# Spare buffers in an edge sort and the pace of an interleaved attention, in a graph-transformer layer

## The chip, the cores and the metric

The kernel runs on one core of one Trainium2 chip. The metric is the device time of one execution in microseconds; the figure given for a kernel is the median of its runs. The core has a tensor engine (TensorE, PE; its weight loads are listed as PEld), a vector engine (VectorE, DVE), a scalar engine (ScalarE, ACT), GpSimd (POOL) and a sync engine (SP) that here only issues transfers.

## The reference

A layer of a graph transformer over 6250 nodes of 256 features and 206,250 directed edges (100,000 drawn, both ways round, and a loop at every node). Cut to what matters:

```python
xn = layernorm(x)
# graph attention, 4 heads of 64
h  = xn @ W;  el = h @ Wl.T;  er = h @ Wr.T
e  = exp(leaky_relu(el[src] + er[dst], 0.2))
w  = e / segment_sum(e, src)[src]
g  = elu(stack_h(segment_sum(w[:, h] * h[dst], src)) + b)
# linear attention, 4 heads of 32, with 4 memory keys and values
q, k, v = split(rmsnorm(xn) @ w_qkv)
m  = rmsnorm((softmax(q) * scale) @ (softmax_n([mem_k, k]).T @ [mem_v, v]) @ w_out + b_out) + xn
x  = x + g + m
# mixture of 8 experts, the best 2 of each token
t  = layernorm(x)
x  = x + t + sum_e(combine[:, e] * (gelu(t @ w1[e] + b1[e]) @ w2[e] + b2[e]))
```

## The kernel before

The nodes are 49 tiles of 128 (NT); the edges lie as 1612 columns of 128 (EC). The work falls into two stages.

**Sort and projections.** The edges have to be brought into the order of their source nodes. `sort_batch` (L364) takes 32 columns at a time, 51 batches in all. Each batch goes through a chain over three engines:

- DVE writes the one-hot `ob` of each edge's pair of node tiles (L381); 32 small matmuls count them into the PSUM tile `n_ps` (L389); a scan on DVE makes running counts `inc` (L393), and a product spreads them into `ahead` (L406).
- Four matmuls give every edge its rank, into `r_ps` (L413, L414), a tile of two PSUM banks. DVE takes the maximum over it into `rank` (L421), and ACT rounds it into `rank2` (L433).
- DVE writes the edges' values times the one-hots into `rv` (two instructions at L438) and the one-hot of the rank, `ohp` (L442), 4096 elements to a partition, the longest instruction of a batch. 32 matmuls over `ohp` and `rv` pack the batch into `g_ps` (L448), and ACT copies it into `grid` (L453).

The SBUF tiles of a batch come from the pool `sortw`, which holds two of each name (`ahead` one); the PSUM tiles of the sort, `n_ps`, `r_ps` and `g_ps`, come from a pool that holds one of each. The projections (`project`, L297) of 13 groups of up to four node tiles run among the first 39 batches: layer norm on ACT and DVE, transposes and matmuls on PE into the PSUM tiles `tp` and `pr` (L337, L342). They write the `table` in HBM that the edges will be gathered from. The last twelve batches run beside `context` (L461), the softmax over all keys and its product with the values. The PSUM pools of this stage are closed at L554 to L556, and the next stage opens its own: among them a one-bank tile `bank` (L840), into which two constants are copied (L850, L851).

**Edges, attention and experts.** For every pair of node tiles, `pack` (L860) brings the edges of the pair into slots, 35 columns to a node tile, and makes the rows `dst_x` to be gathered. `gather` (L949) then issues 35 indirect transfers on POOL into a tile `xe`, of which there are three. When a tile's rows have landed, `weights` (L996) makes the edges' weights, and `sums` (L1009), in four parts, adds the weighted rows into `a_ps` on PE; `look` (L960) prepares the one-hots of the next tile.

The loop of this stage (L1051 to L1076) goes over the node tiles in blocks: nine of four tiles, then smaller ones of 3, 2, 2, 2, 1, 1, 1 and 1. After each of a tile's four parts it calls `some_more` (L1031), which takes one turn (or, in the smaller blocks, as many as it takes to be through at the end of the block) from a list `todo`. First in that list is the `attention` (L568): three turns for each of 13 groups, 39 in all. When the attention has ended, `open_experts` (L624) loads the experts' weights and opens the pool `W["fw"]`; from then on the list holds the `finish_steps` (L654) of the blocks that are through with their sums, each of 11 turns: `front`, `route` and nine turns of expert matmuls (L764, L780). The order of the instructions on each engine is fixed when the program is built.

Of the kernel before, what the change touches and what calls it, by code (L numbers as in the profile page):

```python
# [8 lines left out]
F32 = mybir.dt.float32  # L9
F16 = mybir.dt.float16  # L10
# [7 lines left out]
P = 128  # L18
# [3 lines left out]
BW = 2 * CB  # L22
# [13 lines left out]
def tile_gps_layer(  # L36
# [43 lines left out]
    NB = NQ + NQ % 2  # L80
    BB = min(CB, 512 // NB)
# [116 lines left out]
    def pairs(ap):  # L198

        names = "abcd"[:len(ap.shape) - 2]  # L200
        spaced = " ".join(names)
        return ap.rearrange(f"p {spaced} (n two) -> p {spaced} n two", two=2)
# [11 lines left out]
    sps = sx.enter_context(tc.tile_pool(name="sortp", bufs=1, space=PSUM))  # L214
# [143 lines left out]
    sw = sw_ctx.enter_context(tc.tile_pool(name="sortw", bufs=2))  # L358

    def flat(t):  # L360
        return t.rearrange("p a b -> p (a b)")


    def sort_batch(t):  # L364
        c0 = t * BW
        w = min(BW, EC - c0)
        cs = slice(c0, c0 + w)
        ends = [min(w, a + CB) for a in range(0, w, CB)]
        nb = len(ends)
        bs = slice(t * (BW // CB), t * (BW // CB) + nb)  # L370

        def two(a, n):

            return a[:, :, None, :].to_broadcast([a.shape[0], w, n, 2])

        def row(a, n):

            return pairs(a)[:, None].to_broadcast([a.shape[0], w, n, 2])

        ob = sw.tile([P, BW, NB], F16, name="ob")  # L380
        nc.vector.tensor_tensor(  # L381
            pairs(ob[:, :w]), two(bid[:, cs], NB // 2), row(iota_h[:, :NB], NB // 2),
            op=OP.is_equal,
        )


        n_ps = sps.tile([NB, BW, 2], F32, name="n_ps")
        for c in range(w):
            nc.tensor.matmul(  # L389
                n_ps[:, c, :], lhsT=ob[:, c, :], rhs=one_none, start=True, stop=True  # L390
            )
        inc = sw.tile([NB, BW, 2], F16, name="inc")
        nc.vector.tensor_tensor_scan(  # L393
            flat(inc[:, :w]), starts.rearrange("q b c two -> q (b c two)")[:, :2 * w],
            flat(n_ps[:, :w]), 0.0, op0=OP.mult, op1=OP.add,
        )
        if w == BW:
            nc.scalar.copy(
                ntot[:, bs],
                inc[:NQ].rearrange("q (b c) two -> q b c two", c=CB)[:, :, CB - 1, 0],  # L400
            )
        else:
            for b, e in enumerate(ends):
                nc.scalar.copy(ntot[:, bs][:, b:b + 1], inc[:NQ, e - 1, 0:1])
        ahead = sw.tile([NB, BW, NB], F16, name="ahead", bufs=1)
        nc.vector.tensor_tensor(  # L406
            pairs(ahead[:, :w]), two(inc[:, :w], NB // 2), row(delta, NB // 2), op=OP.mult
        )
        r_ps = sps.tile([P, BW // BB, 512], F32, name="r_ps")
        for i, a in enumerate(range(0, w, BB)):  # L410
            z = min(w, a + BB)
            part = r_ps[:, i, :(z - a) * NB]
            nc.tensor.matmul(part, lhsT=upto_own, rhs=flat(ob[:, a:z]), start=True, stop=False)  # L413
            nc.tensor.matmul(  # L414
                part, lhsT=ones16[:NB, :], rhs=flat(ahead[:, a:z]), start=False, stop=True
            )

        rank = sw.tile([P, BW], F32, name="rank")
        nf = w // BB
        if nf:  # L420
            nc.vector.tensor_reduce(  # L421
                rank[:, :nf * BB].rearrange("p (i c) -> p i c", c=BB),
                r_ps[:, :nf, :BB * NB].rearrange("p i (c b) -> p i c b", b=NB),
                axis=AX.X, op=OP.max,
            )
        if w > nf * BB:
            nc.vector.tensor_reduce(
                rank[:, nf * BB:w],
                r_ps[:, nf, :(w - nf * BB) * NB].rearrange("p (c b) -> p c b", b=NB),
                axis=AX.X, op=OP.max,  # L430
            )
        rank2 = sw.tile([P, BW, 2], F16, name="rank2")
        nc.scalar.activation(  # L433
            rank2[:, :w], rank[:, :w, None].to_broadcast([P, w, 2]), AF.Identity, bias=less_own
        )
        rv = sw.tile([P, BW, 2, NB], F16, name="rv")
        for i, v in enumerate((va, vb)):
            nc.vector.tensor_tensor(  # L438
                pairs(rv[:, :w, i, :]), pairs(ob[:, :w]), two(v[:, cs], NB // 2), op=OP.mult
            )  # L440
        ohp = sw.tile([P, BW, P], F16, name="ohp")
        nc.vector.tensor_tensor(  # L442
            pairs(ohp[:, :w]), two(rank2[:, :w], P // 2), row(iota_h, P // 2), op=OP.is_equal
        )
        g_ps = sps.tile([P, BW // CB, 2, NB], F32, name="g_ps")
        for b, e in enumerate(ends):
            for c in range(b * CB, e):
                nc.tensor.matmul(  # L448
                    flat(g_ps[:, b]), lhsT=ohp[:, c, :], rhs=flat(rv[:, c]),
                    start=(c == b * CB), stop=(c == e - 1),  # L450
                )
        for i in range(2):
            nc.scalar.copy(  # L453
                grid[:, :, bs, i, :],
                g_ps[:, :nb, i, :NQ, None].to_broadcast([P, nb, NQ, 2]).rearrange(
                    "p b q two -> p q b two"
                ),
            )
# [61 lines left out]
    for t0, n in groups:  # L520
        project(t0, n)
        for _ in range(3):
            sort_batch(batches.pop(0))
# [15 lines left out]
    while batches:  # L539
        sort_batch(batches.pop(0))  # L540
        next(steps, None)
# [80 lines left out]
    W = {}  # L622
# [191 lines left out]
    def heads(x2_j, sums, weights):  # L814

        ri = held_pool[0].tile([P, H], F32, name="ri")
        nc.vector.tensor_scalar_max(ri, weights, 1e-12)
        nc.vector.reciprocal(ri, ri)
        nc.vector.tensor_tensor(
            x2_j.rearrange("p (h f) -> p h f", h=H), sums,  # L820
            ri[:, :, None].to_broadcast([P, H, FO]), op=OP.mult,
        )
# [173 lines left out]
    def weights(xe, e_ps):  # L996
        z = gw.tile([P, CPT, H], F32, name="z")
        nc.vector.tensor_reduce(
            z, e_ps[:, 1:].rearrange("p c i h -> p c h i"), axis=AX.X, op=OP.add
        )  # L1000

        tc.keep_in_program_order(nc.vector.tensor_add(z, z, xe[:, :, :H]))  # L1002
        nc.vector.scalar_tensor_tensor(z, z, 0.2, z, op0=OP.mult, op1=OP.max)
        ew = gw.tile([P, CPT, H], F32, name="ew")
        nc.scalar.activation(ew, z, AF.Exp)
        nc.vector.tensor_copy(ew_s, ew)
# [24 lines left out]
    def some_more(calls=None):  # L1031

        steps = 1 if calls is None else -(-sum(max(1, n) for _, n in todo) // calls)
        while todo and steps:
            try:
                next(todo[0][0])
                todo[0][1] -= 1
                steps -= 1
            except StopIteration:
                todo.pop(0)  # L1040
                if "fw" not in W:
                    qx.close()
                    open_experts()
# [7 lines left out]
    for t0, n in blocks:  # L1051
        x2 = gw.tile([P, GT, D], F32, name="x2", bufs=3)
        for j in range(n):
            b = t0 + j
            xe, _ = ready.pop(b)
            oh, e_ps = seen.pop(b)
            weights(xe, e_ps)
            a_ps = pa.tile([FO + 1, S, H, SN], F32, name="a_ps")
            for k in range(S):
                sums(k, oh, xe, a_ps)  # L1060
                if b + 1 < NT:
                    look(b + 1, k)
                if k == 1 and b % U == U - 1 and b + U + 1 < NT:
                    pack(b // U + 2)
                some_more(None if n == GT else (n - j) * S - k)
            a_s = gw.tile([FO + 1, H, S, SN], F32, name="a_s")
            nc.scalar.copy(a_s.rearrange("f h s n -> f s h n"), a_ps)  # L1067
            hd_ps = yps.tile([P, H, FO + 1], F32, name="y_ps")
            for h in range(H):
                nc.tensor.transpose(  # L1070
                    hd_ps[:, h, :], a_s[:, h].rearrange("f s n -> f (s n)"),
                    ident[:FO + 1, :FO + 1],
                )
            heads(x2[:, j, :], hd_ps[:, :, :FO], hd_ps[:, :, FO])
        rows_left = None if (t0 + n) * P <= N else last
        todo.append([finish_steps(hps, yps, x2, t0, n, rows_left, gb_s), NX + 3])  # L1076
# [28 lines left out]
    with tc.If(over_n > 0):  # L1105
        with ExitStack() as gx:
# [45 lines left out]
            with tc.tile_pool(name="allf", bufs=2) as fw, tc.tile_pool(  # L1152
                name="hp2", bufs=2, space=PSUM
# [63 lines left out]
```

## Time and profile before

| what | us |
|---|---|
| runs: median (lowest to highest) | 2762.55 (2759.88 to 2763.56), 3 runs |
| the profiled execution | 2760.09 |
| its span | 2758.0 |
| granted TensorE clock, mean | 0.82 |
| first gather (L952) starts | 443.9 |
| last gather ends | 2635.4 |
| busy: PE, DVE, POOL, ACT | 2108.4, 1939.9, 1688.5, 753.6 |

The profile shows one execution. Busy time of an engine is the time in which one of its instructions ran; a busy PE is not PE at its peak. A group line gives line, engine, operation, tiles written and read, count, then busy time and mean duration in ns, then the engine's idle time just before these instructions and what ended most of it ("<-"). "issue" is time in which the engine waited for nothing that the profile shows. In a list of waits, each line is: who waited, for whom, microseconds in total, how often, and the longest. This is the page's view of the span in 40 equal slices, each digit the busy share in tenths, and PEclk the clock granted to TensorE in tenths:

```profile
PE   6888664556465498969899889596895988887987
DVE  6877977668487668775879568765776676876742
POOL 1000204777777777777677777777777777777610
PEclk9878665666677599979999889698796999888887
```

A slice is 69 us. The first six or seven slices are the sort, the rest is the loop over the node tiles.

### The profile page before, as it was taken

To read this page: it belongs to the slowest core of one execution; us is meant where nothing else is said; L and a number is where in the kernel's file an instruction comes from. 1 tells how busy PE (TensorE), PEld (TensorE's weight loads), DVE (VectorE), ACT (ScalarE), POOL (GpSimd) and SP (SyncE) were. 2 spreads that over 40 slices of the span, in tenths; PEclk is the share of its full clock that TensorE was granted. 3 is DMA by queue.
4 is the path that set the end of the run, shared out by engine and by line. 5 is a ranking of instruction groups with operands and counts; after the bars stand their busy time and mean duration, and the time that the engine had idled before them with its cause. 6 is when DMAs were issued, how large, how long until landed. Compare 5 with 4: busy or idle time off the path is not lost.

```text
span 2758.0 us, 39898 instructions
## 1 busy us (share of the span) xinstructions
PE 2108.4 (76%) x15539; PEld 1584.8 (57%) x15539; DVE 1939.9 (70%) x3992; ACT 753.6 (27%) x1691; POOL 1688.5 (61%) x1779
## 2 busy tenths in 40 slices
PE   6888664556465498969899889596895988887987
PEld 3555442445354367656667667465675666666774
DVE  6877977668487668775879568765776676876742
ACT  4655311112231132213223222021221322232333
POOL 1000204777777777777677777777777777777610
PEclk9878665666677599979999889698796999888887
DMA  2110200222222422121212212212122221221110
GB/s 70 33 30 25 20 1 15 44 59 58 58 59 52 109 36 44 29 44 29 41 29 44 37 36 37 36 29 36 36 29 36 34 40 29 38 37 34 33 15 5
DMA packets 106775, 103.96 MB, mean 38 GB/s; under 512 B 42822, under 2 KB 78884, under 8 KB 106580
## 3 DMA queue, kind: packets, MB, share of 16 engines
q0 software_dynamic: 54880, 60.70, 14.6%
q1 hardware_dynamic: 50004, 39.75, 5.1%
q8 instruction: 124, 2.03, 0.3%
q10 hardware_dynamic: 1696, 0.89, 0.1%
q14 instruction: 71, 0.58, 0.1%
HBM read 86.57 MB, written 14.65 MB: 37 GB/s over the span
## 4 chain that ended last, share of the span: by engine, by line
POOL 29%; PE 26%; DVE 15%; issue 14%; ACT 2%; DMA 2%; DVEq 0%; ACTq 0%; POOLq 0%
POOL xe L952 28%; PE a_ps L1021 8%; PE h_ps L764 7%; PE y_ps L780 6%; DVE rc L914 4%; DVE ohp L919 3%; DVE ohc L907 2%; DMA xe<-table,dst_x 2%; PE y_ps L704 1%; DVE ohw L1014 1%; PE y_ps L755 1%; PE s_ps L924 1%; DVE x L784 1%; POOL kv L492 1%; PE y_ps L699 1%
## 5 line engine op out<-in xcount | busy, mean ns | idle before, releaser
L952 POOL DMA_INDIRECT xe<-table,dst_x x1715 | 1654.5, 965 | 632.7 <-issue 604.4
L1021 PE MATMUL a_ps<-ohw,xe 128*65 128x128 f32 x4410 | 552.1, 283 | 16.3 <-DVE ohw L1014 12.7
L1021 PEld LDWEIGHTS a_ps<-ohw,xe 128*65 128x65 f32 x4410 | 518.2, 144 | 50.9 <-DVE ohw L1014 19.2
L924 PE MATMUL s_ps<-rc,ohp 128*128 128x144 f16 x2525 | 257.4, 275 | 279.7 <-DVE ohp L919 279.6
L764 PE MATMUL h_ps<-tokT,w1s 128*128 128x512 f32 (+3 forms) x1088 | 431.3, 515 | 47.5 <-ACT hT L772 45.4
L924 PEld LDWEIGHTS <-ohp 128*128 128x128 f16 x2525 | 224.7, 121 | 342.9 <-DVE ohp L919 321.5
L780 PE MATMUL y_ps<-w2s,hT 128*128 128x256 f32 x1568 | 405.6, 390 | 0.0
L784 DVE SCALAR_TENSOR_TENSOR x<-y_ps,comb,x 128x256 f32<-128x256 f32 x392 | 189.0, 484 | 230.3 <-PE y_ps L780 230.0
L1014 DVE TENSOR_TENSOR ohw<-oh,bank 128x1280 f32<-128x1280 bf16 x196 | 323.4, 1650 | 32.3 <-PE a_ps L1021 30.8
L780 PEld LDWEIGHTS y_ps<-w2s,hT 128*128 128x128 f32 x1568 | 285.0, 193 | 66.3 <-issue 28.7
L772 ACT ACTIVATE hT<-h_ps,b1s 128x512 f32<-128x512 f32 (+3 forms) x272 | 154.4, 568 | 555.4 <-PE h_ps L764 412.1
L764 PEld LDWEIGHTS h_ps<-tokT,w1s 128*128 128x128 f32 x1088 | 193.6, 205 | 151.3 <-ACT hT L772 79.5
L914 DVE TENSOR_TENSOR rc<-ohc,bank 128x1152 f16<-128x1152 f16 (+1 forms) x350 | 228.0, 693 | 4.5 <-PE s_ps L924 0.7
L919 DVE TENSOR_TENSOR ohp<-to,bank 128x2048 f16<-128x2048 f16 (+1 forms) x175 | 195.1, 1115 | 0.0
L981 ACT COPY ohT<-t_ps 128x768 bf16<-128x768 bf16 x98 | 78.2, 798 | 319.0 <-PE t_ps L977 318.9
L1002 DVE TENSOR_TENSOR z<-z,xe 128x140 f32<-128x140 f32 x49 | 15.0, 307 | 210.6 <-DMA xe<-table,dst_x 202.5
L350 POOL COPY el<-tab 128x16 f32<-128x16 f32 (+1 forms) x13 | 3.5, 267 | 260.7 <-ACT tab L349 260.7
L907 DVE TENSOR_TENSOR ohc<-to,bank 128x1152 f16<-128x1152 f16 (+1 forms) x175 | 121.2, 692 | 0.4 <-ACT to L896 0.4
L442 DVE TENSOR_TENSOR ohp<-rank,iota_h 128x4096 f16<-128x4096 f16 (+1 forms) x51 | 116.1, 2277 | 6.3 <-ACT rank L433 6.0
L342 PE MATMUL pr<-wcat,xT 128*128 128x456 f32 x196 | 109.9, 691 | 5.9 <-ACT xT L339 5.9
L1067 ACT COPY a_s<-a_ps 65x512 f32<-65x512 f32 x49 | 28.4, 580 | 280.6 <-PE a_ps L1021 280.4
L448 PEld LDWEIGHTS <-ohp 128*128 128x128 f16 x1612 | 62.3, 109 | 56.4 <-DVE ohp L442 45.6
(269 smaller groups left out, 2483.9 us busy)
## 6 DMA issues: line engine op xcount, KB each, us to landing
xe<-table,dst_x POOLq DMA_INDIRECT x1715, 2.5
xt<-in_x_dram SPq DMA_DIRECT2D x24, 512.0 KB, 3.9
base_y<-xt SPq DMA_DIRECT2D x12, 512.0 KB
yt<-base_y SPq DMA_DIRECT2D x9, 512.0 KB, 4.4
out_dram<-x SPq DMA_DIRECT2D x9, 512.0 KB
w1s<-in_L_ffn_w_dram SPq DMA_DIRECT2D x8, 256.0 KB
w2s<-in_L_ffn_w_dram SPq DMA_DIRECT2D x8, 256.0 KB, 5.3
table<-tab SPq DMA_DIRECT2D x12, 138.0 KB
```

The source lines that it names most:

```text
L442: nc.vector.tensor_tensor(pairs(ohp[:, :w]), two(rank2[:, :w], P // 2), row(iota_h, P // 2), op=OP.is_equal)
L764: nc.tensor.matmul(h_ps[:, :w], lhsT=w1s[:, e, c, f * P:(f + 1) * P], rhs=held["tokT"][:, c, :w], start=(c == 0), stop=(c == DC - 1),)
L772: nc.scalar.activation(held[e][:, f, :w], h_ps[:, :w], AF.Gelu, bias=b1s[:, k:k + 1])
L780: nc.tensor.matmul(y_ps, lhsT=held[e][:, f, j * P:(j + 1) * P], rhs=w2s[:, e, f, :], start=(f == 0), stop=(f == FC - 1),)
L784: nc.vector.scalar_tensor_tensor(x2[:, j, :], y_ps, held["comb"][:, j, e:e + 1], x2[:, j, :], op0=OP.mult, op1=OP.add,)
L907: nc.vector.tensor_tensor(pairs(ohc[:, :m]), twos(to[:, 0, t0:t0 + m], U * CW // 2), iota_2[:, :, :U * CW // 2].to_broadcast([P, m, U * CW ...
L914: nc.vector.tensor_tensor(pairs(rc[:, :m, i, :]), pairs(ohc[:, :m]), twos(edges_q[:, t0:t0 + m, i, :], U * CW // 2), op=OP.mult,)
L919: nc.vector.tensor_tensor(pairs(ohp[:, :m]), twos(to[:, 1, t0:t0 + m], P // 2), iota_2.to_broadcast([P, m, P // 2, 2]), op=OP.is_equal,)
L924: nc.tensor.matmul(flat(s_ps), lhsT=ohp[:, t - t0, :], rhs=flat(rc[:, t - t0]), start=(t == 0), stop=(t == NBT - 1),)
L952: nc.gpsimd.indirect_dma_start(out=xe[:, c, :], out_offset=None, in_=table, in_offset=bass.IndirectOffsetOnAxis(ap=dst_x[:, c:c + 1], axis=0),
L1014: nc.vector.tensor_tensor(ohw[:, :n], oh[:, g0:g1, i, None, :].to_broadcast([P, n, H, SN]), ew_s[:, c0:c0 + n, :, None].to_broadcast([P, n ...
L1021: nc.tensor.matmul(a_ps[:, i].rearrange("f h n -> f (h n)"), lhsT=xe[:, c, H:], rhs=ohw[:, c - c0].rearrange("p h n -> p (h n)"), start=(c ...
```

## The change

Three tiles of the sort get one more buffer each: `r_ps` two instead of one, `rv` and `ohp` three instead of two. In the loop over the node tiles, `some_more` is called once more after the second and the fourth part of a tile for as long as the experts are not open, so that the attention takes three turns in every two calls instead of two. Nothing else is edited; no instruction is added or taken away.

```diff
-        r_ps = sps.tile([P, BW // BB, 512], F32, name="r_ps")
+        r_ps = sps.tile([P, BW // BB, 512], F32, name="r_ps", bufs=2)
...
-        rv = sw.tile([P, BW, 2, NB], F16, name="rv")
+        rv = sw.tile([P, BW, 2, NB], F16, name="rv", bufs=3)
...
-        ohp = sw.tile([P, BW, P], F16, name="ohp")
+        ohp = sw.tile([P, BW, P], F16, name="ohp", bufs=3)
...
                 some_more(None if n == GT else (n - j) * S - k)
+
+                if k % 2 and "fw" not in W:
+                    some_more()
```

## The prediction

> **What bounds the kernel now.** I read the page's busy shares and costliest groups first, then the timeline of GpSimd (POOL) alone, then the windows by stage, then the waits of the two parts of the sort, and last the timeline of all engines from tile to tile.
>
> ```profile
> PE 2108.4 (76%) x15539; PEld 1584.8 (57%) x15539; DVE 1939.9 (70%) x3992; ACT 753.6 (27%) x1691; POOL 1688.5 (61%) x1779
> L952 POOL DMA_INDIRECT xe<-table,dst_x x1715 | 1654.5, 965 | 632.7 <-issue 604.4
> ```
>
> By busy share TensorE leads. The second line says otherwise: 1715 gathers of 965 ns, and of POOL's 632.7 us of idle time before them 604.4 are "issue", that is, nothing the profile shows held them. The timeline of POOL tells what that issue is:
>
> ```profile
> 443.94 1.14 POOL L952 DMA_INDIRECT xe<-table,dst_x  x1 [95.74 <-issue]
> 448.15 0.94 POOL L952 DMA_INDIRECT xe<-table,dst_x  x1 [0.30 <-issue]
> ...
> 1344.57 0.94 POOL L952 DMA_INDIRECT xe<-table,dst_x  x1 [7.52 <-PE a_ps L1021]
> 2411.05 0.94 POOL L952 DMA_INDIRECT xe<-table,dst_x  x1 [2.60 <-PE a_ps L1021]
> 2592.04 0.94 POOL L952 DMA_INDIRECT xe<-table,dst_x  x1 [5.46 <-PE a_ps L1021]
> 2634.49 0.94 POOL L952 DMA_INDIRECT xe<-table,dst_x  x1 [0.30 <-issue]
> ```
>
> Each gather is followed by 0.30 us of its own issue, and in 2191 us (443.94 to 2635.4) the row is broken only three times, by 15.6 us in all, each time because a gather needed a buffer of xe whose tile was still in its sums (L1021). So the profiled execution of 2760.09 us is 443.9 us up to the first gather, 2191.5 us of gathers one behind the other, 122.6 us of rest after the last, and 2.1 us outside the span of 2758.0. It lies 2.5 us under the median of the runs (2762.55; 2759.88 to 2763.56). In the middle part only POOL's three waits can be won. What is taken from the first part moves the whole row of gathers, and with it the end, one for one.
>
> The first part is the sort (L364 to L458) to 409.7 us, when the last write of the grid starts, and then the first pack, 34 us of DVE work ahead of the first gather, which the change does not touch. How the sort runs:
>
> ```profile
> 100.00:200.00 100.00, 88.84 (x1091) 53.17 (x1090) 78.60 (x126) 61.23 (x241) 1.51 (x10) 0.83 0.12 35
> 200.00:300.00 100.00, 80.00 (x927) 47.07 (x925) 79.64 (x118) 51.87 (x200) 1.62 (x10) 0.81 0.25 30
> 300.00:400.00 100.00, 71.43 (x1021) 50.38 (x1020) 84.51 (x112) 23.21 (x72) 19.03 (x13) 0.62 0.01 2
> ```
>
> The columns are the window, its length, the busy time of PE, PEld, DVE, ACT and POOL, the granted clock, DMA share and GB/s. To 287 us, PE (with the projections of L342) and DVE are both near 80 to 89 with neither full; after it DVE leads. That is two engines that wait for each other in turn:
>
> ```profile
> DVE rv L438 <- PE g_ps L448: 39.7, 28, 4.6
> DVE ob L381 <- PE r_ps L413: 13.6, 10, 3.8
> PE g_ps L448 <- DVE ohp L442: 12.0, 12, 2.4
> PE tp L337 <- ACT xn L332: 5.6, 9, 0.6
> PE pr L342 <- ACT xT L339: 5.4, 12, 0.6
> PE r_ps L413 <- DVE rank L421: 4.1, 9, 0.5
> DVE rank L421 <- PE r_ps L414: 3.8, 6, 1.4
> ```
>
> These are the waits from 30 to 290 us (total, times, longest). The 39.7 us are rv's buffers: its third writer cannot start until the matmuls that read the first are done. From 290 to 410 us the same view has:
>
> ```profile
> PE g_ps L448 <- DVE ohp L442: 24.4, 13, 4.4
> PE r_ps L413 <- DVE rank L421: 13.2, 8, 10.8
> DVE ohp L442 <- ACT rank L433: 6.0, 2, 4.5
> DVE rank L421 <- PE r_ps L414: 5.5, 8, 0.9
> DVE rv L438 <- PE g_ps L448: 4.2, 4, 2.5
> ```
>
> **The change part by part.** No instruction is added or removed; three tags get one more buffer each, and turns of a list of work are taken earlier.
>
> Ranks' sums twice, and rv and ohp thrice, first stage (39 batches, 13 groups, some 21.2 us a group: one rv at 163.96, its like at 185.16). Inside a group PE runs without a gap for the first 11 us while DVE waits for it (2.15, 1.25 and 1.09 us); then DVE runs without a gap for 10 us while PE waits (0.46, 0.95 us, and 1.1 us for the projection's ACT). A third rv and ohp lets DVE go on for one batch's rv and ohp (0.59 + 0.58 + 2.29 = 3.5 us) during the first half, which is less work for it in the second, where PE stands. What goes is PE's waits for DVE: 12.0 + 4.1 = 16.1 us in the window. The 57 us that DVE waits (39.7 + 13.6 + 3.8) are not won, since PE, at 89 of 100, is next in line: late next is the projection's chain through ACT (5.6 + 5.4 us), which I leave in. Lower bound of the gain: nothing, if the engines' fixed order lets DVE only wait at the next instruction. Upper bound: PE also loses its half clock. In windows of 1 us the granted clock is 1.00 from 164 to 176 us and 0.50 from 177 to 183, and so on, group after group; the first projection of a group takes 3.0 us for four matmuls (at 181.28) where the next take 1.8; with g_ps at 1.57 instead of 1.00, r_ps at 0.52 instead of 0.34, and the transposes at 0.69 instead of 0.38, that is some 2.4 us a group, 29 us over 12 groups, so 45 us. DVE, busy 17.0 of 21.2 us, allows that (4.2 x 12 = 50). I take 16, the waits that are measured.
>
> Second part, twelve batches: DVE leads, so its own waits for the two buffers count: 5.5 + 4.2 = 9.7 us. The 6.0 us for ACT's rank stay (ACT was in the exponentials of L493), and so do the 11 us of the maximum at L462, which DVE does itself. Part of each wait only moves to the next one; between nothing and 9.7 I take 5.
>
> The sort's PSUM: tp, pr, n_ps, g_ps one bank each and r_ps two make six of eight; with r_ps twice all eight. The tile named bank is now filled from DVE at 18.60 and 18.85 us (0.22 and 0.18 us), in a bank that the sort does not use; after the change it must wait for one that the sort gives up, at its end on the path: +0.4 us. At best nothing.
>
> Three turns in every two calls, until the experts open. The attention's 39 turns take DVE 121 us, ACT 72 and PE 60 (sums of its groups), so 3.1, 1.9 and 1.5 us a turn; two more a tile are 6.2 us of DVE. What hides them: in tiles 0 to 6 DVE waits 22.2, 12.3, 11.2, 13.2, 0, 17.6 and 21.9 us for the gather (z at L1002), 14 us a tile. If that cover were gone they would make the sums later, but xe has three buffers: the sums of tile 5, the latest, end 7.9 us before the gather of tile 8 needs the buffer. Behind the extra turns stand the sums (k = 2 and the next tile's weights) on DVE and PE, and on SP the loads of xt and stores of base_y, the same in number. The 18 loads of the experts (152 GB/s from 940 to 968 us) come 13 calls, or 3.25 tiles of 44.7 us, earlier; POOL kept its pace under them (21.3 busy of 28 us, as everywhere).
>
> The experts' turns, 11 a block of 16 calls, then start at call 26 instead of 39, one a call. They catch up with the blocks at call 70 (44 turns, tile 17) instead of call 116 (77 turns, tile 29). While they are behind, every call has a turn, and these dense tiles are where the sums lag: with a pack in every odd tile, tiles 11 to 23 end their sums 6.3, 10.9, 7.3, 0.2, 1.1, 10.7 and 10.5 us before POOL needs the buffer, and tile 17 made POOL wait 7.5 us. Dense odd tiles fall from ten to six; 7.5 us in ten becomes 4.5 in six: -3 us. Ends: -7.5 (the wait goes) and +37 (each of the six waits 7.5, less the one there is). The waits at 2411 and 2592 us lie in blocks of fewer tiles, where the list is shared out anew; they stay, as does the rest after the last gather.
>
> Sum: 2760.1 - 16 - 5 + 0.4 - 3 = 2736.5 against the profiled execution, 2739 on the scale of the median.
>
> The Trainium skill speaks against the first part: "TensorE: Matmul & The Clock Gate", HAM oscillation, has a kernel whose PSUM double-buffering gave no further gain. By it the two-fold r_ps would be worth nothing; here its own waits are small too (4.1 and 3.8 us in the first part), so the sum would only rise by a few us, and the weight lies on rv and ohp. The same page holds that the clock falls after an idle window of about 3.4 us and rises after a busy one. By that rule it would not fall in this stage at all, and there would be no clock to win; the rows decide: no PE wait there is over 2.4 us, and the granted clock is 0.83 all the same, so I neither count the clock as won nor rule it out.
>
> **Rivals.**
> - No gain: the sort goes on at PE's pace and DVE's longer lead only moves its wait. For it: PE 88.8 of 100; against it: PE's own 16 us of waits for DVE. Sum 0 to -3 us: 2761. It includes the case that the order of instructions, which is fixed ahead, hardly changes.
> - Larger gain: without pauses PE also keeps its clock: -45 - 9.7 - 7.5: 2700. For it: the slow stretch begins right after the pauses of a group; against it: ACT's pauses (1.1 us a group) remain.
> - Slower: the dense stretch now begins in tiles 7 to 17, and each odd one of these holds the xe buffer too long. Place: the gathers of tiles 10, 12, ... 20 wait for a_ps; price: 37 us, less 21 of the sort: 2762.5 + 37 - 21 + 0.4 = 2779. It decides from 21 us of new POOL waits on. For it: margins of 0.2 and 1.1 us; against it: the other dense margins of 6 to 11 us, with the same work in them.
>
> **How the numbers follow.** The forecast has 0.54, no gain 0.14, larger gain 0.14, slower 0.18. The predicted time is 2739, with a range of its own of 2715 to 2758. Under about 0.2% (5.5 us) a measurement of this kernel does not tell a difference. Faster: 0.50 of the forecast and 0.14, 0.64; same: 0.03 of the forecast and 0.12 of no gain, 0.15; slower: 0.18, 0.01 of the forecast and 0.02 of no gain, 0.21. The range for 8 in 10 goes to 2708 (about half of the larger gain is left out) and to 2768 (some 0.12 of the slower case).
>
> **What would show it.** First gather at 420 to 425 us instead of 443.9; its distance from the last write of the grid still 34 us; the waits of rv for g_ps and of r_ps for rank mostly gone before 290 us; the period of a group under 20.5 us; the gathers' row again about 2190 us long with at most 15 us of waits on a_ps; the first front (L673) some 145 us earlier relative to the first gather; 122 us after the last gather. The prediction is wrong if the first gather does not move, or if POOL waits for a_ps in several of tiles 10 to 20.

## The result, and the profile after

The changed kernel takes 2801.3 us (median of 4 runs, 2796.38 to 2805.3) against 2763.06 us (2759.88 to 2765.48) of the kernel before in runs beside it: a ratio of 1.0138, interval 1.0117 to 1.016. It is slower by 38 us; 2739 us were forecast, and the range ended at 2768.

The profiled execution took 2803.95 us, its span is 2802.1 us, 44.1 longer than before. Divided as in the prediction:

| part | before, us | after, us | difference |
|---|---|---|---|
| up to the first gather | 443.9 | 462.4 | +18.5 |
| row of gathers | 2191.5 | 2217.5 | +26.0 |
| rest after the last gather | 122.6 | 122.2 | -0.4 |

Both places that were to win time lose it. The page's 40 slices of the kernel after, in the same form as before (a slice is now 70 us):

```profile
PE   6898675346647988977959779598695988887887
...
DVE  6767888469966586667766677666776686776742
...
POOL 1000023777777765777777777777777777777710
PEclk9777565667866979997969869699696898888887
```

DVE has 7 and 6 where it had 8 and 7 in the second and third slice; the seventh, in which the gathers start, has 3 for POOL instead of 4; and POOL's row of sevens, unbroken there before, has a 6 and a 5 in the 15th and 16th. First the sort, in three windows (window, length, busy time of PE, PEld, DVE, ACT and POOL, granted clock, DMA share, GB/s):

```profile
100.00:200.00 100.00, 88.47 (x958) 49.91 (x958) 70.83 (x112) 53.65 (x210) 1.22 (x8) 0.74 0.12 33
200.00:300.00 100.00, 87.48 (x937) 49.51 (x935) 70.16 (x115) 55.21 (x218) 1.22 (x8) 0.76 0.09 24
300.00:400.00 100.00, 68.11 (x932) 48.31 (x930) 83.04 (x103) 25.59 (x79) 20.23 (x17) 0.63 0.19 9
```

From 100 to 200 us PE is as busy as before (88.47 against 88.84), but for 958 matmuls instead of 1091, at a granted clock of 0.74 instead of 0.83; DVE does 112 instructions instead of 126. The waits from 30 to 300 us (total, times, longest):

```profile
DVE ob L381 <- PE r_ps L413: 48.0, 22, 4.3
...
ACT xn L332 <- DVE shift L324: 31.5, 10, 3.2
...
DVE rank L421 <- PE r_ps L414: 21.2, 10, 2.2
...
PE g_ps L448 <- DVE ohp L442: 18.0, 11, 1.7
...
PE r_ps L413 <- DVE rank L421: 2.3, 10, 0.8
```

The 39.7 us that rv waited for g_ps are gone from the list. In their place `ob` waits 48.0 us instead of 13.6, `rank` 21.2 instead of 3.8, and ACT's `xn` 31.5 us for a `shift` that it did not wait for before. PE's own waits for DVE, which were to go, are 20.3 us instead of 16.1 (18.0 and 2.3 in this list).

Then the row of gathers. The timeline of POOL (start, duration, what, in brackets the idle time before it and its releaser), all gathers after the first with a wait over 2 us:

```profile
919.90 0.95 POOL L952 DMA_INDIRECT xe<-table,dst_x  x1 [4.50 <-PE a_ps L1021]
...
1015.67 0.95 POOL L952 DMA_INDIRECT xe<-table,dst_x  x1 [8.26 <-PE a_ps L1021]
...
1118.13 0.94 POOL L952 DMA_INDIRECT xe<-table,dst_x  x1 [14.63 <-PE a_ps L1021]
...
1211.50 0.95 POOL L952 DMA_INDIRECT xe<-table,dst_x  x1 [4.00 <-PE a_ps L1021]
...
2455.43 0.94 POOL L952 DMA_INDIRECT xe<-table,dst_x  x1 [2.42 <-PE a_ps L1021]
...
2636.39 0.95 POOL L952 DMA_INDIRECT xe<-table,dst_x  x1 [5.30 <-PE a_ps L1021]
```

Four waits, 31.4 us together, stand at the gathers of tiles 10, 12, 14 and 16, where before had one of 7.52 us (at 1344.57) in the whole dense stretch. The last two were there before, nearly as long. 31.4 - 7.5 is 24 of the 26 us.

### The profile page after: what moved, and what is told of

Read it like the earlier page. It is cut to its first block, busy times and chain, and to the rows that moved or that the text cites. A ratio compares the mean times of both kernels' runs of the same rounds, so it can differ in the third digit from the quotient of the medians.

```text
span 2802.1 us, 39913 instructions
## 1 busy us (share of the span) xinstructions
PE 2141.6 (76%) x15539; PEld 1595.0 (57%) x15539; DVE 1940.8 (69%) x3992; ACT 749.4 (27%) x1688; POOL 1691.5 (60%) x1779
## 4 chain that ended last, share of the span: by engine, by line
PE 33%; POOL 20%; DVE 18%; issue 11%; ACT 3%; DMA 2%; DVEq 0%; ACTq 0%; POOLq 0%
POOL xe L952 20%; PE a_ps L1021 11%; PE h_ps L764 9%; PE y_ps L780 7%; DVE rc L914 5%; DVE ohp L919 4%; DVE ohc L907 2%; DMA xe<-table,dst_x 2%; PE y_ps L704 1%; DVE ohw L1014 1%; PE s_ps L924 1%; PE y_ps L755 1%; DVE inc L878 1%; DVE x L784 1%; ACT hT L772 1%
## 5 line engine op out<-in xcount | busy, mean ns | idle before, releaser
L764 PE MATMUL h_ps<-tokT,w1s 128*128 128x512 f32 (+3 forms) x1088 | 437.3, 522 | 46.8 <-ACT hT L772 44.5
L924 PEld LDWEIGHTS <-ohp 128*128 128x128 f16 x2525 | 219.4, 119 | 303.7 <-DVE ohp L919 282.3
L342 PE MATMUL pr<-wcat,xT 128*128 128x456 f32 x196 | 115.1, 711 | 12.6 <-ACT xT L339 12.6
L448 PE MATMUL g_ps<-rv,ohp 128*128 128x52 f16 x1612 | 67.6, 207 | 44.2 <-DVE ohp L442 43.9
```

Of the source, the lines that this page charges most:

```text
L764: nc.tensor.matmul(h_ps[:, :w], lhsT=w1s[:, e, c, f * P:(f + 1) * P], rhs=held["tokT"][:, c, :w], start=(c == 0), stop=(c == DC - 1),)
L924: nc.tensor.matmul(flat(s_ps), lhsT=ohp[:, t - t0, :], rhs=flat(rc[:, t - t0]), start=(t == 0), stop=(t == NBT - 1),)
```

## The experiments

On the two chips of the runs e1 to e8 all kernels, the one before among them, take some 1.6 ms longer in the loop: 4382 us for the kernel before beside e1 to e4, 4432 beside e5 to e8. The sort ends at the same time there (first gather at 442.7 us in e1_turns, 443.2 in f1_turns, the same kernel), so first gathers can be compared across all runs; the loop only from f1 on, where the kernel before took 2762 to 2765 us. The longer loop is taken up in the last section. A first gather is read from one execution of each kernel. In the ten runs whose sort has the instructions of before in the same order it lies between 442.7 and 446.7 us, so differences of 4 us say nothing.

| run | ratio to before, interval | first gather, us | POOL's waits over 2 us in the row |
|---|---|---|---|
| before | 1 | 443.9 | 15.6 |
| after | 1.0138 (1.0117 to 1.016) | 462.4 | 39.1 |
| e1_turns | 1.0068 (1.0043 to 1.0094) | 442.7 | other chip |
| e2_bufs | 1.0026 (1.0003 to 1.005) | 460.0 | other chip |
| e3_rps | 0.9999 (0.9982 to 1.0017) | 437.9 | other chip |
| e4_rvohp | 1.0026 (1.0007 to 1.0045) | 459.9 | other chip |
| f1_turns | 1.0086 (1.0069 to 1.0103) | 443.2 | 39.6 |
| f2_hold39 | 1.0006 (0.9996 to 1.0016) | 444.9 | 16.6 |
| g1_hold32 | 1.0017 (1.0008 to 1.0027) | 443.5 | 25.1 |
| f3_rv3 | 1.0056 (1.0039 to 1.0073) | 459.6 | 18.5 |
| f4_rv3_ob3 | 0.9947 (0.9923 to 0.9971) | 437.9 | 18.1 |
| g2_turns_xe4 | 1.0063 (1.0047 to 1.008) | 446.1 | 29.3 |
| h1_turns_xe4_early | 0.9952 (0.9938 to 0.9965) | 446.1 | none |
| g3_best3 | 0.9915 (0.9898 to 0.9931) | 416.6 | 15.8 |
| g4_best | 0.9891 (0.9866 to 0.9917) | 421.6 | 7.9 |
| h2_best_early | 0.9877 (0.9858 to 0.9895) | 425.2 | none |

### The change taken apart: e1 to e4, f1, f3

e1_turns and f1_turns are the extra call of `some_more` alone:

```diff
+                if k % 2 and "fw" not in W:
+                    some_more()
```

> Only the three turns in every two calls; the sort's buffers as before. Theory 1 (two losses that add: 18 us in the sort from the buffers, some 26 us in the row of gathers from the turns): the first gather starts at 444 us as before, POOL waits for a_ps at gathers 10, 12, 14 and 16 for 25 to 35 us in all, and the time is 2785 us (2780 to 2792). Theory 2 (the turns cost nothing by themselves; the waits of POOL come from a different phase of the whole loop after the slower sort): POOL waits under 16 us, 2755 to 2766 us.

> Only the three turns in every two calls, a third time, to be read on a chip where the kernel before takes some 2763 us. Theory 1 (losses add): first gather at 444 us, POOL waits 25 to 40 us for a_ps, ratio 1.008 to 1.012. Theory 2 (no loss without the slower sort): POOL waits under 16 us, ratio 0.997 to 1.002. On a chip where the loop is slow as in the runs so far: ratio 1.005 to 1.010 again, which says little of the theories.

e2_bufs has all three buffer edits, e3_rps the first line alone, e4_rvohp the other two, f3_rv3 the second alone:

```diff
+        r_ps = sps.tile([P, BW // BB, 512], F32, name="r_ps", bufs=2)
...
+        rv = sw.tile([P, BW, 2, NB], F16, name="rv", bufs=3)
...
+        ohp = sw.tile([P, BW, P], F16, name="ohp", bufs=3)
```

> Only the three tags' buffers; the turns as before. Theory 1: first gather at 462 us, POOL waits some 16 us as in the kernel before, 2781 us (2776 to 2786). Theory 2: first gather at 462 us and POOL waits near 39 us, 2800 us.

> Only r_ps twice. Theory 1a (the second pair of banks lets PE's fixed order take the first rank matmul of a batch early, and the projections stand behind it): first gather at 455 to 465 us, 2775 to 2785 us. Theory 1b (the third rv and ohp are what upsets the order, and r_ps alone takes away the waits of the rank): first gather at 435 to 445 us, 2753 to 2764 us.

> Only rv and ohp thrice. Theory 1a: first gather at 430 to 445 us, the waits of rv for g_ps gone, 2748 to 2764 us. Theory 1b: first gather at 455 to 465 us, with DVE waiting at ob (L381) for the rank matmuls in place of at rv, 2775 to 2785 us.

> Only the third rv. With ohp thrice alone the order of the instructions on DVE and PE is that of the kernel before, and with rv thrice alone that of rv and ohp thrice. Theory 5 (the third rv alone reorders the sort and costs it 16 to 18 us): first gather at 458 to 462 us. Rival (the third ohp is what costs, through the waits that it takes away): first gather at 440 to 446 us.

The two halves of the loss add up: 1.0086 for the turns and 1.0056 for rv alone make 1.0142, against 1.0138 of the whole change. f1_turns has the four waits of the kernel after at the same gathers (4.89, 6.94, 15.03 and 4.43 us) and its first gather where it was. In the sort, r_ps twice brings the first gather 6 us forward (437.9), rv thrice moves it 16 us back (459.6), and the pair rv and ohp stands at 459.9. So ohp does nothing beside a third rv; alone it was not run. Nor do the gains add: r_ps twice, worth 5 to 8 us alone (437.9 us here, 438.7 in e8_rps_xe4), is worth nothing beside the third rv (460.0 in e2_bufs, 462.4 in the kernel after). With rv thrice the order of the instructions is another: of the 435 DVE instructions of the sort and the projections, 263 stand at another place in the trace than before. The order is the same in f3_rv3 and e4_rvohp.

### The sort: where the wait of rv went, f4

The timeline of DVE and PE in the kernel after, one group's stretch (lines of other tiles left out), shows what late `ob` means:

```profile
155.06 0.58 DVE L438 TENSOR_TENSOR rv<-ob,vb 128x832 f16<-128x832 f16 x1
...
156.75 0.99 PE L448 MATMUL g_ps<-rv,ohp 128*128 128x52 f16 x32
...
157.68 0.34 PE L414 MATMUL r_ps<-ahead,ones 26*128 26x416 f16 x1
...
157.95 1.80 PE L342 MATMUL pr<-wcat,xT 128*128 128x456 f32 x4
...
159.59 0.34 PE L413 MATMUL r_ps<-ob,upto_own 128*128 128x416 f16 x1
...
159.96 0.59 DVE L381 TENSOR_TENSOR ob<-bid,iota_h 128x832 f16<-128x832 f16 x1 [4.31 <-PE r_ps L413]
...
162.15 2.27 DVE L442 TENSOR_TENSOR ohp<-rank,iota_h 128x4096 f16<-128x4096 f16 x1
...
164.48 1.57 PE L448 MATMUL g_ps<-rv,ohp 128*128 128x52 f16 x32 [1.72 <-DVE ohp L442]
...
164.92 0.14 DVE L324 SCALAR_TENSOR_TENSOR shift<-stats,rstd 128x4 f32<-128x4 f32 x1
```

DVE is through with both halves of `rv` at 155.6 and wants to write the next `ob`. There are two of these, and the matmul that reads the older one (L413) stands in PE's queue behind g_ps, one half of r_ps and a projection (L342): it runs at 159.59. So DVE stands 4.31 us with everything that is queued behind `ob` (rank, the next `ohp`, the `shift` of the next group), and PE comes to wait for that `ohp` at 164.48. The wait has gone from one tile to the next. If that is the cause, a third `ob` must take it back.

```diff
+        ob = sw.tile([P, BW, NB], F16, name="ob", bufs=3)
...
+        rv = sw.tile([P, BW, 2, NB], F16, name="rv", bufs=3)
```

> The third rv and a third ob. Theory 6a (with rv free, the next write of ob is what stands, for the rank matmul that reads ob two batches back): the waits at L381 go and the first gather comes at 435 to 450 us. Theory 6b (the loss is in the order, and in the clock that PE is granted between its pauses, not in ob's buffers): first gather at 455 to 465 us.

First f3_rv3, then f4_rv3_ob3, the waits of the sort (from 30 to 300 us):

```profile
DVE ob L381 <- PE r_ps L413: 44.4, 23, 4.0
...
ACT xn L332 <- DVE shift L324: 31.5, 10, 3.2
...
DVE rank L421 <- PE r_ps L414: 22.6, 10, 2.6
```

```profile
DVE rv L438 <- PE g_ps L448: 25.7, 11, 4.1
...
DVE rank L421 <- PE r_ps L414: 15.0, 10, 2.4
...
DVE ob L381 <- PE r_ps L413: 8.3, 6, 2.8
```

The first gather goes from 459.6 to 437.9 us, 21.7 us, `ob` waits 8.3 instead of 44.4 us, and ACT's wait for `shift` has left the list. That a third ob repairs what the third rv broke is shown. Part of the repair may lie in the new order of instructions itself, since a buffer more changes that too; the two were not separated. Nor was a third ob run without the third rv, so what the third rv adds to the pair is open.

The waits are only part of the loss, as the stretch from the first to the 40th `ohp` shows (columns as in the windows above; in order before, after, f3_rv3, f4_rv3_ob3, and three kernels that follow below, g3_best3, g4_best and h2_best_early):

```profile
37.00:324.60 287.60, 241.88 (x2898) 143.14 (x2896) 230.10 (x352) 156.29 (x601) 4.83 (x26) 0.78 0.15 28
...
36.70:347.50 310.80, 260.35 (x2931) 148.63 (x2929) 230.00 (x353) 155.11 (x602) 4.86 (x26) 0.72 0.14 26
...
36.60:342.20 305.60, 255.61 (x2932) 146.91 (x2930) 230.03 (x353) 154.67 (x601) 4.88 (x26) 0.75 0.14 27
...
36.80:324.80 288.00, 251.61 (x2931) 148.15 (x2929) 228.12 (x352) 155.67 (x601) 6.78 (x26) 0.75 0.15 28
...
35.50:303.50 268.00, 232.01 (x2931) 139.39 (x2929) 227.42 (x352) 155.98 (x601) 6.79 (x26) 0.83 0.16 30
...
36.80:309.20 272.40, 236.31 (x2931) 141.57 (x2929) 227.58 (x352) 155.77 (x601) 6.78 (x26) 0.81 0.15 30
...
34.60:312.20 277.60, 241.43 (x2931) 143.81 (x2929) 227.72 (x352) 155.93 (x601) 6.82 (x26) 0.79 0.15 29
```

PE's idle time is the length less its busy time. The kernel after is 23.2 us longer here: 4.7 us more of PE's idle time, and 18.5 us more of busy time for nearly the same matmuls (33 more, about one batch's packing, some 1 us), at a granted clock of 0.72 instead of 0.78. So the larger part of the loss is matmuls that run longer. The third ob takes 13.6 us of PE's idle time away and 4.0 us of its busy time, at the same clock of 0.75 as f3_rv3. That is what it repairs: this stretch is then as long as before (288.0 against 287.6 us), and what f4_rv3_ob3 wins on the kernel before lies in the last batches (from the 40th to the 51st `ohp` 75.1 instead of 83.1 us). Why the clock differs between these kernels is not shown.

### The loop: dense attention or early experts, e5 to e8, f2, g1

The extra call does two things: the attention takes three turns in two calls, and the experts open at call 26 instead of 39. f2_hold39 keeps the first and puts the second back; g1_hold32 opens at call 32, an even tile:

```diff
+        if "fw" not in W and todo[0][1] == 0 and done[0] < 3 * len(groups):
+            return
...
+                done[0] += 1
+                if k % 2 and "fw" not in W:
+                    some_more()
```

(In g1_hold32 the bound is `8 * S`.) e5_turns, e6_hold39 and e7_hold32 are the same three kernels on one of the chips with the longer loop; e8_rps_xe4 has r_ps twice and a fourth `xe`.

> Only the three turns in every two calls, as in the first experiment, which ran on a chip where TensorE stood still so often beside the gathers that the loop over the node tiles took 1.6 ms more. Theory 1 (losses add): first gather at 444 us, POOL waits 25 to 40 us for a_ps, ratio to the kernel before 1.008 to 1.012. Theory 2 (the turns cost nothing without the slower sort): POOL waits under 16 us, ratio 0.997 to 1.002.

> The three turns in every two calls, but the list rests when the attention is through, and the experts open at call 39, as in the kernel before. Theory 3a (what costs is that the experts' turns begin 13 calls early): POOL waits under 16 us, ratio 0.997 to 1.002. Theory 3b (what costs is the denser attention in tiles 0 to 6, which uses up the lead of the gathers): POOL waits 25 to 40 us, ratio 1.008 to 1.012.

> As the one before, but the experts open at call 32, so in the even tile 8 and not in the second half of tile 6. Theory 4a (the opening of the experts, their front and a pack fell into one odd tile, tile 7, which took the margin away): POOL waits under 16 us, ratio 0.997 to 1.003. Theory 4b (dense tiles take longer than the gathers wherever they begin; the earlier they begin, the less lead there is): POOL waits 15 to 35 us, ratio 1.003 to 1.011.

> The kernel before with r_ps twice and a fourth xe. If the waits of POOL are for xe's buffers and the sort gains 5 us from r_ps as in the third experiment: first gather at 438 us, no wait of POOL for a_ps, 2740 to 2748 us, ratio 0.992 to 0.995. If the waits only move (the sums still end as late): ratio 0.996 to 0.999.

> The denser attention with the experts opened at call 39 as before. Theory 3a (the early experts cost): POOL waits under 16 us, ratio 0.997 to 1.002. Theory 3b (the denser attention costs): POOL waits 25 to 40 us, ratio 1.008 to 1.012. On a slow chip: 1.003 to 1.008, undecided.

> The denser attention, and the experts opened at call 32, in the even tile 8, to be read beside a kernel before of some 2763 us. Theory 4a (the opening, the front and a pack in one odd tile took the margin away): POOL waits under 18 us, ratio 0.999 to 1.003. Theory 4b (a dense pair of tiles takes longer than 70 gathers wherever it begins, and the lead is smaller the earlier it begins): POOL waits 20 to 35 us, ratio 1.003 to 1.008.

e5 to e7 came to 1.0071 (1.0045 to 1.0098), 1.0049 (1.0026 to 1.0073) and 1.0091 (1.0057 to 1.0126): the intervals overlap and nothing follows. e8 came to 1.0498 (1.0462 to 1.0534), which belongs to the last section. f2_hold39 decides: 1.0006, with one wait in the dense stretch as before,

```profile
1346.60 0.94 POOL L952 DMA_INDIRECT xe<-table,dst_x  x1 [7.51 <-PE a_ps L1021]
```

and the attention was as dense as in f1_turns (1.0086): its last instruction ends at 811.8 us there and at 810.1 in f1_turns, against 918.3 before. So the denser attention costs nothing that can be measured; the early opening costs all of it. At call 32 it costs about 5 us (2767.94 against 2762.32), with two waits in the dense stretch (8.5 at 1258.62, 4.04 at 1351.81) instead of four. That is between the two theories: the ratio of 1.0017 fits the first, the waits of 25.1 us the second. From call 26 over 32 to 39 the cost falls step by step, so whether it also counts in which tile the list begins is not shown.

### What POOL waits for: g2, h1

If those waits are for a buffer of `xe`, a fourth one takes them away.

```diff
+        xe = gw.tile([P, CPT, TW], F32, name="xe", bufs=4)
```

> The three turns in every two calls with a fourth xe. Theory 7a (the loss of the turns is POOL waiting for xe's buffers, and a fourth one gives 44 us more of lead, more than the lag ever exceeds): no wait of POOL for a_ps in tiles 10 to 16, 2742 to 2752 us, ratio 0.992 to 0.996. Theory 7b (the waits only come later, as TensorE is what is short in those tiles): POOL waits over 20 us, ratio 1.002 to 1.008.

It took away the first (gather 10) and the two late ones (2434 and 2615 us in f1_turns), but at gathers 12, 14 and 16 waits of 6.22, 17.89 and 5.14 us stayed, so the first theory fails; the second has the size, but not the reason. The timeline of g2_turns_xe4 tells it (DVE's last write of `dst_x`, then POOL; before the second, ACT's last copy out of a_ps, into `a_s`, with which a tile's sums are through):

```profile
991.51 0.19 DVE L935 TENSOR_SCALAR dst_x<-dst_x 128x72 int32<-128x72 int32 x1
...
992.45 1.77 POOL L952 DMA_INDIRECT xe<-table,dst_x  x1 [6.22 <-issue]
...
1016.38 0.57 ACT L1070 COPY a_s<-a_ps 65x512 f32<-65x512 f32 x1
...
1098.56 0.18 DVE L935 TENSOR_SCALAR dst_x<-dst_x 128x72 int32<-128x72 int32 x1
...
1099.48 0.94 POOL L952 DMA_INDIRECT xe<-table,dst_x  x1 [17.89 <-PE a_ps L1021]
...
1192.50 0.18 DVE L935 TENSOR_SCALAR dst_x<-dst_x 128x72 int32<-128x72 int32 x1
...
1193.42 0.94 POOL L952 DMA_INDIRECT xe<-table,dst_x  x1 [5.14 <-PE a_ps L1021]
```

Each of the three gathers starts 0.74 or 0.75 us after the end of that instruction, while the last `a_s` before it had ended 50.5, 82.5 and 77.9 us earlier. The profile names a_ps as the releaser of two of them, but the buffers had long been free: here POOL waits for the rows to be gathered, which `pack` makes in the odd tile. In the kernel after the same writes end 2.85 to 8.0 us ahead of the four gathers, and a_ps ends with the gather; so there the buffer ends last, and the rows stand close behind. h1_turns_xe4_early adds to g2 that the packing of a pair is taken a tile earlier, in the even tile:

```diff
-                if k == 1 and b % U == U - 1 and b + U + 1 < NT:
+                if k == 1 and b % U == 0 and b + U + 2 < NT:
...
+            loc = gw.tile([P, GC, S, 2], BF16, name="loc", bufs=6)
```

> The turns' extra call alone with a fourth xe, as in g2_turns_xe4, and with the packing of a pair taken in the even tile (one tile earlier), loc six times. In g2_turns_xe4 POOL starts the gathers at 992.45, 1099.48 and 1193.42 us some 0.75 us after DVE has written their dst_x, and 50 to 82 us after the a_s of the tile before, so theory one: with four buffers what POOL waits for is the destinations that the packing of the odd tile makes, and the three waits of 29 us together are for nothing else. It expects them under 3 us together, and a ratio to the kernel before of 0.993 to 0.998 (before has 15.6 us of waits that would be gone too). Theory two: the dense attention delays the sums themselves, and the packing taken earlier only moves the delay into the gathers' weights and the sums. It expects waits of 15 us or more still, or as much time between the last gather and the end, and a ratio of 1.003 or more.

Theory one held. The groups of h1_turns_xe4_early have:

```profile
L952 POOL DMA_INDIRECT xe<-table,dst_x x1715 | 1649.6, 962 | 620.8 <-issue 608.9 <-DMA xe<-table,dst_x 6.7 <-PE y_ps L751 1.2
```

No wait for a_ps or dst_x is left among the releasers shown, the row takes 2172.0 us instead of 2191.5, and the ratio is 0.9952: the same turns that cost 0.9% with three buffers and the packing in the odd tile. The kernel before with these two edits and without the turns was not run, so a gain is not shown for the turns, only that they no longer cost. Of the 19.5 us that the row loses, 10.2 come back behind it: the rest after the last gather is 132.8 us instead of 122.6, and so it is, on the chips with the short loop, in every kernel with a fourth xe (128.1 to 132.8 us). What holds the end there was not looked into.

### The best of it: g3, g4, h2

g3_best3 has r_ps twice, rv and ob thrice, and the turns as before; g4_best adds the fourth `xe`, h2_best_early also the packing a tile earlier (with the edits shown).

> The kernel before with r_ps twice, rv thrice and ob thrice. If the third ob is what the third rv needed: first gather at 432 to 440 us, ratio 0.992 to 0.998. If r_ps twice upsets that order again: first gather over 443 us, ratio over 0.999.

> The same with a fourth xe. If both gains add (some 8 to 10 us in the sort, 15 us of POOL's waits): ratio 0.989 to 0.993, 2735 to 2745 us, no wait of POOL for a_ps. If the sums' lag moves to the end of the loop instead: ratio 0.994 to 0.998.

> r_ps twice, rv and ob three times, xe four times, as in g4_best, with the packing of a pair in the even tile and loc six times. Theory one: the one wait that g4_best has left (7.9 us at 1321.17, 0.75 us after its dst_x) goes, and nothing takes its place: ratio 0.985 to 0.989 to the kernel before. Theory two: the packing taken earlier collides with the list in the early tiles, or the experts' opening then falls on another wait: ratio 0.989 or more.

g3_best3 brings the first gather to 416.6 us, 27 us forward and further than expected, with the row of before (2191.0 us), and 2737.49 us against 2762.32. The profile caught the fastest of its four executions, though: 2728.18 us, 9 us under the median. The windows of its sort:

```profile
100.00:200.00 100.00, 92.16 (x1180) 55.22 (x1178) 85.68 (x138) 68.00 (x266) 3.06 (x12) 0.91 0.13 37
200.00:300.00 100.00, 77.63 (x949) 46.81 (x950) 83.98 (x121) 42.93 (x164) 2.04 (x8) 0.70 0.22 24
```

From 100 to 200 us 1180 matmuls and 138 DVE instructions run instead of 1091 and 126, at a granted clock of 0.91 instead of 0.83; from 200 to 300 us the clock is 0.70 instead of 0.81. The sort gains what the change was expected to win there, by another set of buffers. The fourth xe and the earlier packing then empty the row of its waits (15.8, 7.9 and none), but the rest after the last gather comes to 128.1 and 132.3 us, and the intervals of the three (0.9915, 0.9891, 0.9877) overlap in turn. Their sorts have the same instructions in the same order, and from the first to the 40th `ohp` the same idle time of PE (36.0, 36.1 and 36.2 us in the lines above); yet the first gather comes at 416.6, 421.6 and 425.2 us, since PE is busy for 232, 236 and 241 us at a granted clock of 0.83, 0.81 and 0.79. So the 27 us are 18 to 27 from one execution to another. h2_best_early at 2731.23 us (2727.59 to 2735.69) is the fastest measured, 1.2% under the kernel before; it has neither the third ohp nor the extra turns.

## Why the prediction was wrong

Two terms of the sum failed, both in sign; the division into three parts, and most of what was said to stay, held.

**Held.** The last grid write is 34.4 us ahead of the first gather (34.3 before). The rest after the last gather is 122.2 us. The last part of the sort won what was taken, from the 40th to the 51st `ohp` 78.5 us instead of 83.1, that is 4.6 for the forecast 5; but in part by luck. DVE's waits for rv, rank and ob there fell only from 8.5 to 6.9 us (rv's went, ob's came with 3.4); some 2.4 us were won because DVE was busy for 64.3 instead of 66.7 us there, having written part of its tiles before. The bank's copies moved to 428.33 us, right behind the last grid write, and cost the path 0.1 us instead of 0.4. The first front comes at 836.95, 374.6 us after the first gather instead of 524.0: 149 us earlier for the forecast 145. The extra turns of attention are hidden (f2_hold39).

**"What goes is PE's waits for DVE: 16.1 us".** This failed. The first 39 batches became 22.9 us longer (the 40th `ohp` starts at 347.5 instead of 324.6). I had let DVE run ahead by the `rv` and `ohp` of one batch and looked no further than those two tiles. But `ob` also has only two, is written once a batch and is read late by a matmul deep in PE's queue, so DVE ran ahead into that: ob's 13.6 us, which I had in the list and left there, became 48.0, and with it stopped `shift`, which ACT and the next projection need. I named "the projection's chain through ACT" as late next, and left it at its old 11 us. So PE's idle time did not fall by 16.1 us but rose by 4.7. The sum had no term at all for the larger part: it counted PE's busy time as given, or shorter, and that rose by 18.5 us at a granted clock of 0.72 instead of 0.78. The lower bound "nothing" was wrong as well: it held the order of the instructions for given, and a third rv changes it, so a loss belonged into the range. The third rv alone makes the step fail (f3_rv3); r_ps twice is worth 5 to 8 us alone and nothing beside it, and the third ohp nothing beside it.

**"7.5 us in ten becomes 4.5 in six: -3 us".** This failed: the row became 26 us longer. The term spread the one wait of before evenly over the dense odd tiles and counted the tiles. The margins of before, 0.2 to 11 us in tiles 11 to 23, are no property of a dense tile: opened at another call, the same work in tiles 7 to 13 had no margin. Whether that is because of where in the list's round of turns each `pack` falls, or because the gathers have less of a lead the earlier the list begins, the runs do not separate. The result lies within the stated ends of this term, -7.5 and +37. The rival **Slower** had the place and the first half of the mechanism: gathers of tiles 10 to 16 wait for a_ps, 31.4 us in four waits (it said six, 37 us more than before). Its total of 2779 was 22 us too low, since it granted the sort a gain of 21 us where the sort lost 18.5, and priced the waits too high. What neither the term nor the rival saw is the second condition behind the buffer: the rows of the next pair come from the same odd tile, and end 3 to 8 us before the gather.

**The rivals.** "No gain" put the sort at 0 to -3 us and "larger gain" at -45: both fell. The buffers of g3_best3 win 18 to 27 us there (the first gathers of the three kernels with them), between the two.

**The clock.** The prediction neither counted nor ruled out a won clock; it was lost: 0.74 and 0.76 instead of 0.83 and 0.81, with no wait of PE in the list over 1.7 us. The Trainium skill ("TensorE: Matmul & The Clock Gate", What's actually happening) holds that the clock halves after an idle window of about 3.4 us. No such window shows here in the waits, and the clock fell all the same. The runs do not tell whether the lower clock is a consequence of the late `ob`; but the third ob won back 17.6 us up to the 40th `ohp` at the same clock of 0.75, so that repair is not a won clock.

The Trainium skill also says ("Perfetto Trace Analysis", Optimization Strategy) that the same gap repeating on the engine that should be saturated can mean too few buffers. The trace agrees with the reading, as rv's 39.7 us went with a third rv; but the gap was on DVE, busy for 79 of 100 us from 100 to 200 us before, and not on PE, busy for 89, and its end cost 16 us.

## What to carry to other kernels

A buffer added where a wait shows lets the engine run on only to its next two-buffered tile: follow the queue past that wait, tile by tile, before you decide which of them get one (first gather with rv alone +16 us, with ob -6, with ob and r_ps -18 to -27). A stage's loss need not stand in its waits: compare the busy time of the engine that leads, and its granted clock, over the same work. Where the order of instructions is fixed when the program is built, a buffer more also changes that order, so "nothing" is not the lower end of its gain. Where work is pulled forward in an interleaved loop, look for every condition of the transfer that sets the pace, since a free buffer and ready indices may come from the same late tile; with a fourth xe and the packing a tile earlier, the kernel with the same turns was 0.5% faster than the one before instead of 0.9% slower.

## What the runs showed of the hardware

Two chips ran the kernel before in 4382 and 4432 us instead of 2763, the sort as fast as elsewhere. Each chip was used in one round of runs only. There PE, DVE and ACT stand still together for stretches in which POOL issues gathers without a break, and POOL then waits in its turn (in e8_rps_xe4 24 waits over 2 us, 1888 us together, where the kernel before on a short loop has 15.6). A stretch of e8_rps_xe4 (the timeline of all engines; idle time in brackets):

```profile
906.81 1.75 DVE L1014 TENSOR_TENSOR ohw<-oh,bank 128x1536 f32<-128x1536 bf16 x1 [45.05 <-remote]
...
909.67 0.27 ACT L590 COPY qT<-y_ps 128x128 f32<-128x128 f32 x1 [48.89 <-remote]
...
909.99 1.22 PE L592 MATMUL y_ps<-cw,qT 128*128 128x256 f32 x2 [47.46 <-issue]
```

From 862 to 905 us the transfers of this run are of one queue, in the view of DMA:

```profile
q0 software_dynamic: 1094, 1.20, 16.0%
```

In the same window the kernel before, on a chip with the short loop, has 1087 packets of that queue, 528 of q1 and two each of q8 and q14, whose kind is "instruction". Engines that stand still ask for less, so this may be what follows from the standstill and not its reason. On that chip r_ps twice and a fourth xe, which lets POOL issue longer without a pause, made the kernel 5% slower; on the chips with the short loop a fourth xe made it no slower (g2_turns_xe4 beside f1_turns, g4_best beside g3_best3). What holds the engines there, and why only on some chips, no run here tests.
